# Adapter and output weights turned by VectorE and moved through DRAM, with an early reordering of the start, in a LoRA and paged-attention kernel

## The chip, the cores and the metric

The kernel runs on one core of one Trainium2 chip. The metric is the device time of one execution in microseconds (us). A core has several engines with a queue of instructions each: TensorE (PE in the profile; PEld is its weight load), VectorE (DVE), ScalarE (ACT), GpSimd (POOL) and SyncE (SP). DMA transfers are issued from the queues of SP, ACT and POOL. An engine executes its queue in order, so an instruction that waits holds up everything behind it on that engine.

## The reference, cut to what matters

For 8 batches of 128 tokens of width 512, all in float32:

```python
# layer 0: each batch has its own adapter, a 512 x 512 matrix out of 16
w = weight[adapter_ids]
x = x + einsum('bsi,boi->bso', x, w)

# layer 1: attention over a paged cache of 512 keys and the 128 new ones
q = rope(rmsnorm(x @ Wq.T, q_norm_w))      # 32 heads of 128
k = rope(rmsnorm(x @ Wk.T, k_norm_w))      # 8 heads of 128
v = x @ Wv.T
kc, vc = k_cache[block_table], v_cache[block_table]     # 16 pages of 32
scores = q . concat(kc, k) / sqrt(128), keys past the batch's length masked
o = softmax(scores) . concat(vc, v)
x = x + o @ Wo.T
```

All weights lie in DRAM with the output index first, so each 128 x 512 block of rows has to be turned (transposed) before TensorE can use it.

## The kernel before

**Steps and slots.** The work is cut into 32 steps: 4 groups of heads (g) times 8 batches (b), `steps = [(g, b) ...]`, group by group. A step handles 8 query heads and 2 key heads of one batch and has 8 slots, one for each query head. A slot begins with the matmuls of that head's scores (`sc`, line 1040; two buffers in PSUM). VectorE adds the mask and takes the minimum (L1050), ScalarE takes the exponential (L1066), VectorE inverts the sum (L1106), GpSimd scales (L1113), and one slot later VectorE turns the probabilities in blocks of 32 x 32 (`turn_p`, L886). SP's DMAs (`exchange`, L806) bring the blocks to their places (`pT`).

**The planner.** Between the score matmuls TensorE gets a list of pieces, `main`: the projections of the next step (`pj_kv`, `pj_q`), the probabilities times values of the step before (`values`, tile `o`), the output of the step before (`output`, tile `out`), and in group 0 the adapter product of a later batch (`lora_y`, tile `y`). A matmul piece has a cost of 0.86 (`UNIT`), a transpose 0.11 (`TR`). Beside them stand `turns`, transposes with a fixed slot (`at(step, slot, early, f)`; early ones come ahead of the exponential, the others after the slot's pieces). In each slot the planner hands out pieces as long as they fit its share:

```python
ahead = sum(c for k in range(h + 1, 8) for _, c, _ in turns_at.get((i, k), []))
mine = sum(t[1] for t in turns)
share = (sum(c for c, _ in main) + ahead + mine) / (8 - h) - mine
while main and (h == 7 or took + main[0][0] / 2 <= share):
```

Copies and additions that follow a group of matmuls are put into `pending` and emitted at the next `run(pending)`.

**Turning weights.** There are two ways. `turn_weights`, `turn_lora` and `turn_lora_row` use four TensorE transposes into a PSUM buffer (`ps_mm`, a ring of four; `spare` takes one of the two `sc` buffers), and one copy out of it by ScalarE or VectorE. All weights of group 0 and all adapters are turned so. The other way serves groups 1 to 3: `send_weights` has VectorE turn 32 x 32 blocks (L513) into a `facing` tile and returns the DMA that writes it to DRAM, emitted a slot later from the ACT queue (`to_write`); `receive_weights` reads it back from the same queue, many slots later. The slots of the turns stand in `turn_when`, those of the reads in `reads_at`; after each turn `load_next` fetches the next block of weights.

**Adapters.** The row of adapter numbers selects the adapter. Adapters 0 and 1 are loaded by SP; `gather_lora` (POOL, L239) gathers the others, 1 MB each, into a single buffer `lraw`. In step i of group 0 `turn_lora(i + 2, c)` turns adapter i + 2, one chunk c in each of four slots; `lora_y(i + 2)` multiplies, an addition updates `acc`, and `turn_x1(i + 2)` turns the result for the projections. `turn_x(b)` turns x itself ahead of that.

**Unused space.** The output weights of group 0 (`o0`, `o1`) wait from the start in the tiles of batches 4 to 7 (`acc`, `x1T`), until these are needed.

**The start.** Ahead of step 0 the order is written out by hand: a small row (lengths, block table, adapter numbers, norm weights) is spread over the partitions by two tiny matmuls (`spread`, L391), from it come rope tables and gather indices; x, the first weights and adapters 0 and 1 are turned, step 0 is projected, and the cached keys of step 0 are turned by TensorE (`turn_kc`, L763, copies L766).

Of the kernel before, what the change touches and what calls it, by code (L numbers as in the profile page):

```python
# [18 lines left out]
P = 128  # L19
# [33 lines left out]
def lora_then_paged_attention(  # L53
# [28 lines left out]
    facing = pool("facing", 2)  # L82
# [121 lines left out]
    wn = const.tile([P, 2, D], FP, name="wn")  # L204
# [53 lines left out]
    for i, (g, b) in enumerate(steps):  # L258
        if i == 0:
            at(i, 2, False, lambda: turn_q(0, 1))  # L260
            at(i, 7, False, lambda: turn_q(1, 0))
            for n, h in enumerate((7, 8, 9, 10)):
                at(i, h, False, lambda n=n: turn_weights(("o1", 0, n)))
# [12 lines left out]
        if g == 0 and b + 2 < B:  # L276
            at(i, 0, True, lambda b=b: turn_x(b + 2))
            for c in range(KC):
                at(i, c if i else c + 2, False, lambda b=b, c=c: turn_lora(b + 2, c))
            at(i, 8 if i else 9, True, lambda b=b: turn_x1(b + 2))  # L280
    for turns in turns_at.values():
        turns.sort(key=lambda t: not t[0])

# [6 lines left out]

    for g in range(1, G):
        before = 8 * B * (g - 1)
        for k, kind in enumerate(("kv", "q0", "q1")):
            for n in range(4):
                turn_when[before + 9 + 5 * (4 * k + n) // 2] = len(turns_of)
                turns_of.append((kind, g, n))
                read_at(before + 8 * (B - 2) + (2, 4, 6)[k] + n, (kind, g, n))
        for n, slot in enumerate((39, 42, 45, 62, 64, 66, 68, 70)):
# [95 lines left out]
    def rope_angles():  # L394
# [20 lines left out]
        nc.vector.tensor_scalar(turns, turns, ROUND, None, ALU.subtract)  # L415
        for part in (TWO_PI_1, TWO_PI_2, TWO_PI_3):
# [6 lines left out]
    def row_rest():  # L423

        nc.vector.tensor_copy(row_f[:, at_bt:at_wn], row_i[:, at_bt:at_wn])
# [26 lines left out]
    def rope_table(n):  # L452
        sin, cos = rope["sin"], rope["cos"]
        if n == 0:
# [5 lines left out]
        nc.vector.tensor_tensor(SW[:, n, :, H2:D], sin, w1, ALU.mult)  # L460
        nc.vector.scalar_tensor_tensor(
            out=SW[:, n, :, 0:H2], in0=sin, scalar=-1.0, in1=w2, op0=ALU.mult, op1=ALU.mult
        )
        nc.vector.tensor_tensor(CW[:, n, :, 0:H2], cos, w1, ALU.mult)
        nc.vector.tensor_tensor(CW[:, n, :, H2:D], cos, w2, ALU.mult)
# [7 lines left out]
    def transposed(name, blocks, dsts, copy=None, spare=False):  # L473
# [8 lines left out]
        for dst, lo, n in dsts:  # L482
            (copy or nc.scalar.copy)(dst, t[:, lo : lo + n, :])  # L483
# [26 lines left out]
    def send_weights(kind, a, n):  # L510

        t = facing.tile([P, 4, 4, Q4], FP, tag="tw", name=f"tw_{kind}_{a}_{n}")
        nc.vector.transpose(t, raw.pop((kind, a, n)).rearrange("p (c i a) -> p a c i", c=4, a=4))  # L513
# [7 lines left out]
    def receive_weights(kind, a, n):  # L521
        if n == 0:
            wT[kind] = wts.tile([P, 4, 4, 4, Q4], FP, tag=kind, name=f"w_{kind}_{a}")
        nc.scalar.dma_start(
            out=wT[kind][:, n, :, :, :].rearrange("p b c j -> p b (c j)"),
# [3 lines left out]
    def turn_lora(b, c, copy=None, spare=False):  # L529

        if c == 0:
            wT["lora"] = lora.tile([P, KC, 4, P], FP, tag="wT", name=f"wT_{b}")
# [4 lines left out]
            [(wT["lora"][:, c, :, :], 0, 4)],  # L537
# [4 lines left out]
    def turn_lora_row(b, j, copy):  # L542

        if j == 0:
            wT["lora"] = lora.tile([P, KC, 4, P], FP, tag="wT", name=f"wT_{b}")
        rows = lraw[b].rearrange("p (j i) -> p j i", j=4)
        transposed(f"lw_{b}_{j}", chunks(rows[:, j, :]), [(wT["lora"][:, :, j, :], 0, 4)], copy)


    def turn_x(b, copy=None):  # L550
        transposed(f"x_{b}", chunks(acc[b]), [(x1T[b], 0, 4)], copy)

    def turn_x1(b, copy=None):
        transposed(f"x1_{b}", chunks(acc[b]), [(x1T[b], 0, 4)], copy)
# [32 lines left out]
    def lora_y(b):  # L587
        def after(y):
            def add():
                a = acc[b].rearrange("s (p j) -> s j p", j=4)  # L590
                nc.vector.tensor_tensor(a, y.rearrange("s (j p) -> s j p", j=4), a, ALU.add)
# [6 lines left out]
                lambda c=c: (x1T[b][:, c, :], wT["lora"][:, c, :, :].rearrange("k j p -> k (j p)"))  # L598
# [334 lines left out]
    table_set(AF.Sin)  # L933
    rope_angles()
    turn_x(0, on_act)
    for n in (2, 3, 0, 1):
        turn_weights(("kv", 0, n), on_act)
    rope_sin()
# [252 lines left out]
```

## Time and profile before

| | |
|---|---|
| time, median of 3 runs | 1193.76 us (1192.11 to 1201.34) |
| the profiled execution's own time | 1193.18 us |
| its span, first to last instruction | 1191.3 us |
| TensorE busy | 1172.7 us, 98% of the span |
| VectorE, ScalarE, GpSimd busy | 743.9, 534.0, 674.1 us |
| DMA moved | 217.59 MB, mean 183 GB/s |
| first score matmul of step 0 | 40.75 us |

In lists of waits a row names who waited for whom, with the total in us, the number of times and the longest. In a timeline a row has its start, its length, engine, line, operation, `out<-in`, shapes and count, and in brackets how long the engine stood idle before it and what ended that. Rows of a timeline can overlap a little, since an engine starts the next instruction before the one ahead has drained. In a table by stage each engine's busy time in us is followed by its number of instructions. "Clock" is the granted TensorE clock, 1.00 at full speed.

### The profile page before, as it was taken

The page shows a single profiled execution, that of the slowest core. Times are in us where ns is not written, and L with a number is a line of the kernel's source. Part 1 is how long each engine was busy: PE and PEld are TensorE (multiplying, and loading weights), DVE is VectorE, ACT ScalarE, POOL GpSimd, SP SyncE. Part 2 cuts the span into 40 slices and gives each one's busy share as a digit, 9 for nine tenths or more (in the row PEclk, how much of TensorE's full clock was granted, in tenths as well). Part 3 has the DMA queues.
Part 4 walks back from the last instruction along what each step waited for, and adds up shares of the span by engine and source line. Part 5 has one row for each costly group of instructions (what it writes and reads, how often), then busy time and mean ns, then how long its engine had stood idle before and what let it go on. Part 6 is the DMA issues. An engine that isn't in the chain of part 4 may idle for free.

```text
span 1191.3 us, 13375 instructions
## 1 busy us (share of the span) xinstructions
PE 1172.7 (98%) x3354; PEld 572.0 (48%) x3354; DVE 743.9 (62%) x1675; ACT 534.0 (45%) x1648; POOL 674.1 (57%) x780
## 2 busy tenths in 40 slices
PE   7899999999999999999999999999999999999998
PEld 4555454454444444444444444444444444444454
DVE  5566566565667676666666676676666656665651
ACT  4564444444444444444444444444444444444432
POOL 5565346455666565656655556565555656655540
PEclk9999999999999999999999999999999999999999
DMA  8277577766867977786777978766777875665642
GB/s 291 100 180 197 135 220 206 172 180 168 226 173 189 253 192 191 191 215 169 199 187 180 258 198 216 196 175 171 190 203 178 219 180 148 148 153 135 152 111 59
DMA packets 173952, 217.59 MB, mean 183 GB/s; under 512 B 19508, under 2 KB 112436, under 8 KB 172980
## 3 DMA queue, kind: packets, MB, share of 16 engines
q1 hardware_dynamic: 111072, 128.76, 46.8%
q10 hardware_dynamic: 49524, 48.12, 12.7%
q0 software_dynamic: 13280, 39.86, 10.4%
q8 instruction: 28, 0.46, 0.2%
q14 instruction: 48, 0.39, 0.1%
HBM read 80.74 MB, written 17.83 MB: 83 GB/s over the span
## 4 chain that ended last, share of the span: by engine, by line
PE 96%; POOL 1%; DMA 1%; ACT 1%; DVE 1%; issue 1%; DVEq 0%; ACTq 0%; POOLq 0%
PE sc L1040 23%; PE o L566 23%; PE pj_q L566 18%; PE out L566 18%; PE pj_kv L566 9%; PE y L566 2%; PE lw L481 1%; DMA lraw<-in_L_cond_weight_dram,lora_ix 1%; PE x L481 1%; PE wt_q L499 0%; PE wt_kv L499 0%; PE qt L793 0%; PE wt_o L499 0%; POOL kc L617 0%; POOL vc L617 0%
## 5 line engine op out<-in xcount | busy, mean ns | idle before, releaser
L1050 DVE CUSTOM_DVE_ANT_0 p<-sc,mask 128x640 f32<-128x640 f32 x256 | 210.9, 824 | 381.2 <-PE sc L1040 380.9
L1066 ACT ACTIVATE p<-p,mn 128x640 f32<-128x640 f32 x256 | 212.0, 828 | 331.8 <-DVE mn L1050 328.0
L1113 POOL TENSOR_SCALAR p<-p,rc 128x640 f32<-128x640 f32 x252 | 201.5, 800 | 235.3 <-DVE rc L1106 230.9
L1040 PE MATMUL sc<-kT,qT 128*128 128x512 f32 (+1 forms) x1024 | 319.5, 434 | 1.1 <-ACT kT L773 0.8
L1040 PEld LDWEIGHTS sc<-kT,qT 128*128 128x128 f32 x1024 | 192.7, 191 | 232.5 <-issue 225.7
L566 PE MATMUL pj_q<-w_q,x1T 128*128 128x512 f32 x512 | 236.8, 593 | 0.7 <-ACT w_q L500 0.7
L566 PE MATMUL o<-pT,vc 128*128 128x512 f32 x512 | 237.1, 593 | 0.0
L566 PE MATMUL out<-w_o,oT 128*128 128x512 f32 (+1 forms) x528 | 234.9, 580 | 0.9 <-ACT oT L853 0.7
L886 DVE STREAM_TRANSPOSE tp<-p 128x640 f32<-128x640 f32 x252 | 210.8, 837 | 4.0 <-POOL p L1113 3.8
L685 POOL TENSOR_TENSOR q<-q,sw 128x512 f32<-128x512 f32 (+1 forms) x89 | 96.6, 1086 | 98.8 <-DVE sw L668 98.6
L617 POOL DMA_INDIRECT kc<-in_L_cond_k_cache_dram,key_ix x128 | 130.7, 1021 | 32.7 <-issue 32.5
L617 POOL DMA_INDIRECT vc<-in_L_cond_v_cache_dram,val_ix x128 | 127.3, 995 | 31.2 <-issue 29.8
L566 PEld LDWEIGHTS out<-w_o,oT 128*128 128x128 f32 x528 | 95.7, 190 | 93.5 <-issue 85.4
L566 PEld LDWEIGHTS pj_q<-w_q,x1T 128*128 128x128 f32 x512 | 92.4, 190 | 92.7 <-issue 90.6
L698 ACT ACTIVATE q<-q,rs 128x128 f32<-128x128 f32 x256 | 81.8, 390 | 118.1 <-POOL q L685 102.2
L566 PEld LDWEIGHTS o<-pT,vc 128*128 128x128 f32 x512 | 92.2, 191 | 88.5 <-issue 86.4
L566 PE MATMUL pj_kv<-w_kv,x1T 128*128 128x512 f32 x256 | 116.6, 593 | 0.7 <-ACT x1T L483 0.7
L651 ACT ACTIVATE sq<-pj_q 128x128 f32<-128x128 f32 x256 | 70.6, 276 | 57.5 <-PE pj_q L566 41.6
L693 POOL TENSOR_TENSOR rs<-ss,mhalf 128x6 f32<-128x6 f32 x64 | 77.3, 1207 | 5.3
L566 PEld LDWEIGHTS pj_kv<-w_kv,x1T 128*128 128x128 f32 x256 | 46.0, 190 | 45.6 <-issue 44.7
L566 PE MATMUL o<-pT,vn 128*128 128x512 f32 x128 | 65.4, 593 | 0.0
L651 ACT ACTIVATION_READ_ACCUMULATOR sq<-pj_q 128x1 f32 x256 | 49.7, 194 | 0.0
(123 smaller groups left out, 811.5 us busy)
## 6 DMA issues: line engine op xcount, KB each, us to landing
pT<-tp SPq DMA_DIRECT2D x252, 320.0 KB, 6.1
kT<-tk SPq DMA_DIRECT2D x248, 64.0 KB, 2.9
qT<-tq SPq DMA_DIRECT2D x116, 96.0 KB, 2.7
qT<-tq SPq DMA_DIRECT2D x120, 64.0 KB, 4.0
st_q<-in_L_cond_Wq_dram ACTq DMA_DIRECT2D x24, 256.0 KB, 5.5
xw_q<-tw_q ACTq DMA_DIRECT2D x24, 256.0 KB, 5.5
st_o<-in_L_cond_Wo_dram ACTq DMA_DIRECT2D x24, 256.0 KB, 5.7
xw_o<-tw_o ACTq DMA_DIRECT2D x24, 256.0 KB, 6.5
```

Of the source, the lines that this page charges most:

```text
L481: nc.tensor.transpose(t[:, j, :], blk, ident)
L566: nc.tensor.matmul(y[0], lhsT=lhsT, rhs=rhs, start=(k == 0), stop=(k == len(pieces) - 1))
L617: nc.gpsimd.indirect_dma_start(out=dst[:, c, :], out_offset=None, in_=src, in_offset=bass.IndirectOffsetOnAxis(ap=rows[:, g, at : at + 1], ...
L651: nc.scalar.activation(sq, t[:, h, :], AF.Square, scale=float(D) ** -0.5, accum_out=ss[:, h : h + 1])
L685: add.tensor_tensor(dst, cw, sw[:, 0:heads, :], ALU.add)
L693: nc.gpsimd.tensor_tensor(rs[:, 0:width], ss[:, 0:width], mhalf[:, 0:width], ALU.pow)
L698: nc.scalar.activation(q, q, AF.Identity, scale=rs[:, h : h + 1])
L886: nc.vector.transpose(u.tp[:, :, r, :], u.p.pop(r).rearrange("q (a k) -> q a k", a=4))
L1040: nc.tensor.matmul(sc[:, lo:hi], lhsT=s.qT[j][:, r, 0:4, :].rearrange("d h q -> d (h q)"), rhs=s.kT[j].rearrange("d a c i -> d (a c i)")[: ...
L1050: nc.vector.tensor_tensor_reduce(out=p, in0=sc[:, 0:LA], in1=mask.rearrange("p a c i -> p (a c i)"), scale=1.0, scalar=3.0e38, op0=ALU.add ...
L1066: nc.scalar.activation(p, p, AF.Exp, bias=unit.mn[:, one], scale=-1.0, accum_out=unit.sm[:, one])
L1113: nc.gpsimd.tensor_scalar(q, p, unit.rc[:, one], 1.0, ALU.mult, ALU.mult)
```

## The change

- **The start.** x of batch 0 and two blocks of kv weights are turned ahead of the first small spread, and two rows of adapter 0 ahead of the second. The sine and cosine tables come after the gather of keys; `rope_table(1)` is split into its sine and cosine halves. The last two q1 weight blocks are turned between the kv and the q0 projection; the q1 projection and its `run(pending)` now stand ahead of the key gather of step 1 and of `turn_kc`. `row_tables` and the mask move later.
- **Step 0.** The four o0 blocks come one after the other, `turn_x1(1)` after all of them.
- **Adapters 4 to 7 and o1 of group 0** go through `send_weights` and `receive_weights`, in the slots of `extra`; each read stands two slots after its write. Adapter 3 stays with TensorE, two chunks a slot. The adapter's turned tile gets the layout of the other weights, `[P, 4, 4, KC, Q4]`.
- **Around it.** `gather_lora(b + 3)` moves from the end of slot 6 to the end of slot 2, `load_x(b + 3)` to slot 4 (step 0 keeps slot 6); `turn_x1(7)` comes a slot earlier; turns of group 1's weights move to slots that `extra` leaves free; `facing` has three buffers, and `wn` shares the tile `tk`.

```diff
@@ turns
+            at(i, 6, False, lambda: row_tables(range(1, G)), 0)
             at(i, 7, False, lambda: turn_q(1, 0))
-            for n, h in enumerate((7, 8, 9, 10)):
-                at(i, h, False, lambda n=n: turn_weights(("o1", 0, n)))
...
-            for c in range(KC):
-                at(i, c if i else c + 2, False, lambda b=b, c=c: turn_lora(b + 2, c))
-            at(i, 8 if i else 9, True, lambda b=b: turn_x1(b + 2))
+            if i < 2:
+                for c in range(KC):
+                    at(i, c // 2 if i else c + 2, False, lambda b=b, c=c: turn_lora(b + 2, c))
+            at(i, (7 if b + 3 == B else 8) if i else 9, True, lambda b=b: turn_x1(b + 2))
@@ slots of turns and reads
+    extra = {}
+    for n, slot in enumerate((5, 6, 7, 8)):
+        extra[slot] = ("o1", 0, n)
+        read_at(slot + 3, ("o1", 0, n))
+    for b in range(4, B):
+        for j, slot in enumerate((8, 8, 9, 10)):
+            extra[8 * (b - 3) + 4 + j] = ("lora", b, j)
+            read_at(8 * (b - 3) + slot, ("lora", b, j))
...
+                if g == 1:
+                    slot = (9, 10, 11, 17, 18, 24, 25, 26, 32, 33, 34, 40)[4 * k + n]
...
-        for n, slot in enumerate((39, 42, 45, 62, 64, 66, 68, 70)):
+        for n, slot in enumerate((42, 44, 46, 62, 64, 66, 68, 70)):
@@ send_weights, receive_weights
-        nc.vector.transpose(t, raw.pop((kind, a, n)).rearrange("p (c i a) -> p a c i", c=4, a=4))
+        rows = lraw[a][:, n * HID : (n + 1) * HID] if kind == "lora" else raw.pop((kind, a, n))
+        nc.vector.transpose(t, rows.rearrange("p (c i a) -> p a c i", c=4, a=4))
...
+            pl, tag = (lora, "wT") if kind == "lora" else (wts, kind)
+            wT[kind] = pl.tile([P, 4, 4, 4, Q4], FP, tag=tag, name=f"w_{kind}_{a}")
+        dst = wT[kind][:, :, n, :, :] if kind == "lora" else wT[kind][:, n, :, :, :]
@@ start
     row_parts()
     table_set(AF.Sin)
+    turn_x(0, on_act)
+    for n in range(2):
+        turn_weights(("kv", 0, n), on_act)
     rope_angles()
-    turn_x(0, on_act)
-    for n in (2, 3, 0, 1):
+    for n in range(2, 4):
         turn_weights(("kv", 0, n), on_act)
-    rope_sin()
+    for j in range(2):
+        turn_lora_row(0, j, on_act)
     row_rest()
-    for j in range(4):
+    for j in range(2, 4):
         turn_lora_row(0, j, (on_act, on_vec)[j % 2])
...
     for _, f in project(0, "kv"):
         f()
+    for n in range(2, 4):
+        turn_weights(("q1", 0, n), on_act)
     rope_table(0)
     run(pending)
     for _, f in project(0, "q0"):
         f()
+    make_mask(0)
     run(pending)
-    for j in range(GK):
-        turn_kc(0, j, on_vec)
-    for n in range(2, 4):
-        turn_weights(("q1", 0, n), on_act)
+    for _, f in project(0, "q1"):
+        f()
     run(pending)
     for c in range(LC):
         gather_k(1, c)
-    row_tables(range(1, G))
-    for _, f in project(0, "q1"):
-        f()
+    for j in range(GK):
+        turn_kc(0, j, on_vec)
     turn_x(1, on_vec)
     for c in range(KC):
         turn_lora(1, c, on_vec if c % 2 else on_act, True)
     gather_lora(2)
+    turn_k(0, 0, on_act)
     turn_q(0, 0, on_act)
-    turn_k(0, 0, on_act)
@@ step 0 and the loop
-                if n == 2:
+                if n < 4:
+                    turn_weights(("o0", 0, n))
+                else:
                     turn_x1(1)
-                turn_weights(("o0", 0, n))
-            main += [(4 * TR * (1 + n // 2), lambda n=n: second(n)) for n in range(3)]
-            main += [(4 * TR, lambda: turn_weights(("o0", 0, 3)))]
+            main += [(4 * TR, lambda n=n: second(n)) for n in range(5)]
...
+            if 8 * i + h in extra:
+                to_write.append(send_weights(*extra[8 * i + h]))
...
-            if g == 0 and h == 6 and b + 3 < B:
-                load_x(b + 3)
-                gather_lora(b + 3)
+            if g == 0 and b + 3 < B:
+                if h == (4 if i else 6):
+                    load_x(b + 3)
+                if h == (2 if i else 6):
+                    gather_lora(b + 3)
```

## Prediction

> **What bounds it now.** I read the busy shares first, then the waits of TensorE (PE), then busy time by stage, then the timelines of PE and VectorE (DVE) at the start.
>
> ```profile
> PE 1172.7 (98%) x3354; PEld 572.0 (48%) x3354; DVE 743.9 (62%) x1675; ACT 534.0 (45%) x1648; POOL 674.1 (57%) x780
> ```
>
> PE is busy for all but 18.6 us of the span. Only two things can shorten the kernel: instructions taken from PE, and the few waits that PE has. They stand in the list of waits (total, times, longest):
>
> ```profile
> PE spread L391 <- DVE row_f L395: 6.1, 1, 6.1
> PE lw L481 <- DMA lraw<-in_L_cond_weight_dram,lora_ix: 2.4, 1, 2.4
> PE x L481 <- DVE rc L1106: 0.9, 1, 0.9
> ...
> PE pj_kv L566 <- ACT x1T L483: 0.7, 1, 0.7
> ```
>
> The start of each step (its first sc matmul in PE's timeline) gives stages: the first at 40.75, step 0 33.4 us long, step 1 42.0, step 2 44.7, steps 3 to 5 40.5 each, step 6 35.8, and 34.4 from step 7 on. Columns are PE, PEld, DVE, ACT, POOL busy, clock, DMA share, GB/s; the rows are steps 2, 3 and 9:
>
> ```profile
> 116.13:160.87 44.74, 42.34 (x126) 21.10 (x125) 25.57 (x53) 18.33 (x55) 21.55 (x25) 0.96 0.65 178
> 160.87:201.33 40.46, 40.46 (x125) 20.18 (x124) 25.29 (x55) 18.42 (x55) 21.53 (x25) 1.00 0.74 194
> ...
> 386.85:421.25 34.40, 34.40 (x93) 16.23 (x92) 23.59 (x52) 15.01 (x49) 19.63 (x23) 1.00 0.93 249
> ```
>
> Step 3 has no idle PE at all, so what is taken from PE there is time. Step 2 loses 4.27 us against it: 2.40 of waiting for the gathered adapter, and the rest by the clock, which is 0.5 for 3.41 us after that wait. Its matmuls show it: four of sc take 2.34 us, elsewhere 1.24.
>
> ```profile
> 123.22 1.03 PE L481 MATMUL lw<-ident,lraw 128*128 128x128 f32 x4 [2.40 <-DMA lraw<-in_L_cond_weight_dram,lora_ix]
> 124.05 2.34 PE L1040 MATMUL sc<-kT,qT 128*128 128x512 f32 x4
> ```
>
> **Term A, adapters 4 to 7 leave PE: -7.0.** In each of steps 2 to 5 four groups of four transposes go; a group moves the next instruction by 0.436 us (lw at 129.88, sc at 130.32). 16 x 0.436 = 7.0. In exchange come, for these and the o1 rows of term B, 20 turns on DVE, 20 writes and 20 reads on the ACT queue.
>
> - DVE: 20 x 1.06 us (L513) = 21 us, 4.2 a step. It is busy 25.3 of 40.46 us in step 3 and waits 1 to 3 us a slot for sc; with 29.5 of 38.7 it still fits, and the fullest slot (rotation, mask, p turn and one weight turn, 198.10 to 202.39) took 4.3 us. Price 0.
> - DVE may wait for the gather: it is issued after slot 2's p, 6.1 us into that slot, and lands 5.8 to 9.1 us later (rows of lraw); the turn in slot 4 comes some 13.3 us after slot 2's start. That is 0 to 2 us, with the reciprocal and the next mask operation queued behind. PE is a slot ahead in two sc buffers: 0.
> - ACT loses 20 copies of 0.585 us and gets 40 issues, 0.33 for a write, 0.37 to 3.06 for a read. A read waits for its write; two slots are 9 us, the longest such write took 7.4. Behind a late one stand the exp and all that follows it. In steps 7 to 30 such reads run with no PE wait: 0.
> - DMA: the ACT queue took 12.7% of the span for 48.12 MB, 3.1 us per MB; 2.1 MB more in a step of 38.7 us is 0.17. 0.74 x 40.5/38.7 + 0.17 = 0.94. Step 9 ran at 0.93 without a PE wait: 0, but this is the edge, and rival 2.
> - Moves: the gather goes ahead of the two key gathers of slot 3 on POOL, 0.94 + 0.3 us of issue; x (0.4 us on SP) goes ahead of the pT transfer of slot 5 instead of the next step's. Each has slots to spare: 0.
>
> **Term B, second output weights (o1) leave PE: -1.3.** Four groups of 0.436. The three in step 1 count. The one that closed step 0 covered the qT copy of the next step: sc waited 0.24 us there with it, and waits 0.68 without.
>
> **Term C, the wait of step 2: -4.3.** Adapter 4 is no longer PE's; 44.74 goes to 40.47 before term A. **Term D, step 6: -0.7**, because x1 of batch 7 is turned a slot earlier, ahead of its kv projection.
>
> **Term E, the start: +2.5.** PE's first transposes can begin at some 4.0 (x and the first weights land at 3.9 and 4.8), not 6.06, but adapter 0's second half lands at 12.3 whatever the order, so y starts near 14.05 instead of 15.44. With two more weight turns now ahead of q0, the q0 projection ends at 29.05 (29.41 before) and q1 right after, at 32.55 (36.61 before): 4 us gained on PE. Then the new order bites. Before, q1's rotation ran in slot 0; now it stands ahead of the kct copies on DVE, and a rotation starts only when ACT's squares are done:
>
> ```profile
> 31.09 0.69 DVE L664 TENSOR_TENSOR q<-pj_q,CW 128x512 f32<-128x512 f32 x1 [3.20 <-ACT sq L651]
> 31.70 0.74 DVE L668 TENSOR_TENSOR sw<-pj_q,SW 128x256 f32<-128x256 f32 x2
> 32.48 0.69 DVE L685 TENSOR_TENSOR q<-q,sw 128x512 f32<-128x512 f32 x1
> 33.08 1.28 DVE L766 COPY kT<-kct 128x512 f32<-128x512 f32 x2
> ```
>
> Queue by queue, from 29.05: ACT squares q0 to 30.7; DVE rotates it (2.08) to 32.8; ACT scales it (1.28) to 34.2 and squares q1 (1.56) to 35.8; DVE rotates q1 to 37.9, copies kct (1.28) to 39.1, x (0.62) to 39.8, adapter 1's second chunk (0.65) to 40.4; PE turns the fourth chunk, which needs that buffer, to 40.9, then k and q; ACT copies both to 42.15. So sc starts at 42.15, +1.4. PE idles 3.5 us before that fourth chunk; after 2.40 us the clock halved, so I add 1.1 for turns and sc at half clock. Bounds: -4.1 (all of the q1 gain kept) to +3.5 (3.41 us at half clock cost 1.7 on top of 1.4, plus 0.4 for the later gathers).
>
> **Term F, step 0: +1.6.** The planner in the loop hands PE its pieces by cost. In slot 1 it now has one y piece and five 0.44 turns. Before, the test passed for all (2.84 against 20.12/7 = 2.874); with the o1 turn gone the share is 19.68/7 = 2.811, and x1 of batch 1 falls into slot 2, directly ahead of the kv projection that reads it. Its copy is queued on ACT behind the exp of slot 2: mask 1.29 us after the slot's start, exp at 2.15, copy 2.98 to 3.56, kv at 3.65; PE is ready at 1.75. Wait 1.9. In slot 1 the fourth o0 turn needs the buffer that the y addition frees: 0.6. The old 0.93 wait goes. 1.9 + 0.6 - 0.9 = 1.6. Whether 1.9 us also halves the clock (+1.7) lies between two rows: 0.93 did not, 2.40 did; I take no. Bounds: -0.9 to +3.3.
>
> [...]
>
> **Term G, adapter 3 in step 1: +1.0.** It is still PE's, now both first groups in slot 0, and no o1 turn stands ahead. Before, it landed at 78.20 and was used at 78.77. Without the 0.44 the margin is 0.1 us, and the writes of o1 share the DMA: one 256 KB write is about 1 us. Bounds 0 (landing in 5.8) to 5.0 (in 9.1: 3.3, and 1.7 of clock).
>
> **Term H, adapter 7: +0.3.** In step 5 its y comes in slot 3, 6.46 us after slot 2's start; its last read is issued at 2.25 in slot 2 and lands 4.3 to 4.8 us later (w_q, w_o). Bounds 0 to 2.
>
> **Sum.** -7.0 - 1.3 - 4.3 - 0.7 + 2.5 + 1.6 + 1.0 + 0.3 = -7.9. The profiled execution took 1193.18 us (span 1191.3), 0.6 under the median of the runs, 1193.76. 1193.2 - 7.9 = 1185.3. About 1% is what a measurement of this kernel can tell from no change: faster is below 1181.8, slower above 1205.7.
>
> **Rivals.**
> 1. *The start pays* (chance 0.21). The DVE chain of term E overlaps better than I queue it and 3 of the 4 us stay; x1's copy is in time. -13.3 - 3.0 + 0.5 = -15.8: 1177.4. For it: q1 ends 4 us earlier. Against: the order on DVE and ACT is in the code.
> 2. *The round trip is late* (0.07), the other side. From slot 2's read to y are 8.8 us for adapters 4 to 6, 4.2 for 7. If reads take 12 us, PE waits 3 x 3.2 + 7.8 = 17.4 and each of four waits costs 1.7 of clock: 1185.3 + 17.4 + 6.8 = 1209.5. For it: a DMA share of 0.94 over five steps in a row. Against: step 9, and no weight read or write above 7.4.
> 3. *The moved turns bound DVE* (0.07): steps 2 to 5 stay at 40.5 because a slot's DVE work passes the slot, so term A does not appear. 1185.3 + 7.0 = 1192.3. Against: 29.5 of 38.7.
>
> [...]
>
> **Chances.** Forecast 0.65, rivals 0.21, 0.07, 0.07. Faster by over 1%: rival 1 and 0.04 of the forecast's own spread, 0.25. Slower by over 1%: 0.06 of rival 2. Within: 0.69. The bounds add to 1175 and 1194; both ends at once are unlikely below, so the range is 1178 to 1194.
>
> **What would show it.** Right: steps 3 and 4 last 38.7 us with full PE, no lw wait in step 2, the first sc near 42 to 43.5 with an idle PE before the fourth lw of adapter 1, a kv wait for x1T in slot 2 of step 0 near 1.9, few tenths at lw in step 1. Wrong: a first sc before 40, PE waits for wT in steps 2 to 5, DVE waits there that reach sc.

## The result and the profile after

The changed kernel takes 1208.05 us (median of 4 runs, 1205.59 to 1210.23) against 1192.98 for the kernel before on the same chip: a ratio of 1.0113, 95% interval 1.0087 to 1.0139 (the medians alone give 1.0126). It is slower by 1.1%, where 1185.3 was forecast, in a range of 1178 to 1194. Its profiled execution took 1205.59 us (span 1203.8), 12.4 more than the 1193.18 of before.

The engines' line of the page after:

```profile
PE 1171.9 (97%) x3274; PEld 565.7 (47%) x3274; DVE 757.4 (63%) x1694; ACT 522.8 (43%) x1629; POOL 673.1 (56%) x780
```

TensorE has 80 instructions fewer, but only 0.8 us less busy time: once the clock has first been full, five stretches of 3.41 us at half clock (from 14.76, 42.06, 86.44, 144.46 and 229.80 us) lengthen its matmuls, where the kernel before had one (from 123.30). The span is longer by 12.5 us, and 31.9 us of it are idle, 18.6 before. The waits of PE after (total, times, longest):

```profile
PE o L590 <- DMA pT<-tp: 5.7, 3, 2.5
...
PE lw L498 <- DMA lraw<-in_L_cond_weight_dram,lora_ix: 2.7, 1, 2.7
PE o L590 <- issue: 2.4, 1, 2.4
PE y L590 <- DMA w_lora<-xw_lora: 2.2, 1, 2.2
...
PE pj_kv L590 <- ACT x1T L501: 1.8, 1, 1.8
PE sc L1069 <- ACT kT L803: 1.6, 1, 1.6
```

Before, `o` (probabilities times values) did not wait at all. Now it waits in each of steps 1 to 4, 0.73, 2.41, 2.40 and 2.52 us, for `pT`, the probabilities that VectorE has turned and SP's DMAs spread. (The 2.40 stands under "issue", as the trace shows no event at its end.) Steps 2, 3 and 9 by stage, with PE, PEld, DVE, ACT, POOL, clock, DMA share and GB/s:

```profile
125.07:168.13 43.06, 40.65 (x110) 19.11 (x108) 27.49 (x58) 16.12 (x51) 21.56 (x25) 0.96 0.81 218
168.13:209.47 41.34, 38.94 (x109) 18.54 (x108) 28.33 (x59) 16.24 (x51) 21.52 (x25) 1.00 0.85 238
...
399.33:433.73 34.40, 34.40 (x93) 16.23 (x92) 23.48 (x52) 15.11 (x49) 19.54 (x23) 1.00 0.92 251
```

Step 3 has 38.94 us of PE work where 38.7 was forecast, but lasts 41.34. From step 7 on nothing differs: step 7 starts at 318.04 us before and at 330.53 after. By stage, against before:

| stage | forecast | measured |
|---|---|---|
| start and step 0 (E, F) | +4.1 | +4.8 |
| step 1 (B, G) | -0.3 | +4.2 |
| steps 2 to 4 (A, C) | -9.5 | +1.9 |
| step 5 (A, H) | -1.4 | +2.9 |
| step 6 (D) | -0.7 | -1.3 |

**Why `pT` can be late.** A step's probabilities come in two units, and up to step 4 both use one buffer of `pT`. Until the values of the first unit have been multiplied, SP cannot issue the second. SP's rows in step 3 before (start 160.87) and after (168.13):

```profile
164.95 2.51 SPq L806 DMA_DIRECT2D qT<-tq  x4
168.83 5.53 SPq L806 DMA_DIRECT2D pT<-tp  x4
```

```profile
172.22 2.49 SPq L831 DMA_DIRECT2D qT<-tq  x4
175.65 5.04 SPq L831 DMA_DIRECT2D pT<-tp  x4
```

SP begins 8.0 us after the step's start before, 7.5 after. PE wants the result 17.7 us after the start before:

```profile
178.54 1.88 PE L566 MATMUL o<-pT,vc 128*128 128x512 f32 x4
```

It landed at 17.1 to 17.3 in steps 3 to 5, so in steps 3 and 4 the margin was about half a microsecond (in step 5 PE wants it later). After, without the adapter's transposes, PE is there at 16.5 us, and the landing has moved to about 18.8. Counted from the issue, PE leaves 9.0 us instead of 9.7, and the transfer takes 11.2 and 11.5 in steps 2 and 4 instead of 9.2 to 9.3. So 0.7 us of the wait are the transposes that PE no longer does meanwhile, and the larger part is the slower transfer. The wait of step 2, which starts at 125.07:

```profile
144.00 4.51 PE L590 MATMUL o<-pT,vc 128*128 128x512 f32 x6 [2.41 <-DMA pT<-tp]
```

(144.00 is 18.93 us after 125.07; six matmuls take 4.51 us at a clock of 0.50 from 144.46 on, where they take 2.81 in step 3.) The DMA engines in these 11 us (7.5 to 18.5 of step 3), by queue with packets, MB and share; q1 is SP's queue, q10 ScalarE's. Before, then after:

```profile
DMA packets 1216, 2.01 MB, mean 183 GB/s; under 512 B 135, under 2 KB 440, under 8 KB 1216
...
q1 hardware_dynamic: 920, 1.47, 64.3%
q10 hardware_dynamic: 296, 0.54, 12.8%
```

```profile
DMA packets 2165, 2.78 MB, mean 253 GB/s; under 512 B 161, under 2 KB 1208, under 8 KB 2161
...
q1 hardware_dynamic: 704, 1.37, 56.1%
q10 hardware_dynamic: 1457, 1.38, 37.6%
```

ScalarE's queue moves 1.38 MB there instead of 0.54, and the share of all queues goes from 77% to 95%, while over the whole step after it is 85%.

### The profile page after: what moved, and what is told of

Read it like the earlier page. It is cut to its first block, busy times and chain, and to the rows that moved or that the text cites. A ratio compares the mean times of both kernels' runs of the same rounds, so it can differ in the third digit from the quotient of the medians.

```text
span 1203.8 us, 13251 instructions
## 1 busy us (share of the span) xinstructions
PE 1171.9 (97%) x3274; PEld 565.7 (47%) x3274; DVE 757.4 (63%) x1694; ACT 522.8 (43%) x1629; POOL 673.1 (56%) x780
## 4 chain that ended last, share of the span: by engine, by line
PE 89%; DMA 5%; SPq 1%; DVE 1%; POOL 1%; issue 1%; ACT 1%; ACTq 0%; POOLq 0%; DVEq 0%
PE o L590 23%; PE sc L1069 22%; PE out L590 18%; PE pj_q L590 16%; PE pj_kv L590 8%; DMA pT<-tp 3%; PE y L590 2%; SPq L831 1%; DMA lraw<-in_L_cond_weight_dram,lora_ix 1%; DMA qT<-tq 1%; DMA raw_lora<-in_L_cond_weight_dram 1%; DMA w_lora<-xw_lora 1%; PE x L498 0%; POOL kc L642 0%; SPq L160 0%
## 5 line engine op out<-in xcount | busy, mean ns | idle before, releaser
L590 PE MATMUL o<-pT,vc 128*128 128x512 f32 x512 | 240.0, 600 | 8.1 <-DMA pT<-tp 5.7
L717 POOL TENSOR_SCALAR ss<-ss 128x6 f32<-128x6 f32 x64 | 13.0, 203 | 69.2 <-ACT sq L676 67.7
```

Of the source, the lines that this page charges most:

```text
L590: nc.tensor.matmul(y[0], lhsT=lhsT, rhs=rhs, start=(k == 0), stop=(k == len(pieces) - 1))
L717: nc.gpsimd.tensor_scalar(ss[:, 0:width], ss[:, 0:width], EPS, 1.0, ALU.add, ALU.mult)
```

## Experiments

Where no ratio is given the time is that of one execution; the kernel before took 1191.54 us beside the first four runs (e1 to e3) and 1191.19 beside e4 to e7. Single times of one and the same kernel differ by up to 12 us (f1, below), so what these runs tell is read from the waits in their profiles.

### Which traffic makes pT late

**e1_no_gather**: VectorE turns a constant, and adapters 4 to 7 are not gathered.

```diff
-        rows = lraw[a][:, n * HID : (n + 1) * HID] if kind == "lora" else ...
+        rows = key_no.rearrange("p a c j -> p (a c j)") if kind == "lora" else ...
-                    gather_lora(b + 3)
+                    if b == 0:
+                        gather_lora(b + 3)
```

> The changed kernel without the gathers of adapters 4 to 7: VectorE turns a constant in their place, everything that follows (writes, reads, products) is kept, so batches 4 to 7 get a wrong adapter. In the changed kernel the pT transfer of unit 1 in steps 2 to 4 starts 7.5 us into the step, when the values of unit 0 have been read out of the single pT buffer, and lands at 18.7; TensorE is ready for it at 16.5 and waits 2.4. The 1 MB gather starts at 15.2, in the middle of this transfer. Theory 'moved gather': the transfer shrinks to the 9.2 us of before, the waits fall to 0.2 to 0.5, steps 2 to 4 take about 39 us instead of 43.1, 41.4, 43.2, the whole about 1195. Theory 'round trip': the writes and reads in slots 0 to 2 slow the transfer, the gather does not, the waits stay at 2 to 2.4.

1205.94 us. The waits of steps 1 to 4 stay: 1.33, 1.98, 2.65, 2.28. Without the gather ScalarE's queue still moves 0.95 to 1.43 MB in the 11 us.

**e1b_no_gather_two_buffers**: the same, and the first unit's `pT` in the adapter's idle buffer, so that the second need not wait for it.

```diff
-        pl, tag = (lora, "raw") if u.j == 0 and u.i >= B - 3 else (pts, "pT")
+        pl, tag = (lora, "raw") if u.j == 0 and u.i >= 1 else (pts, "pT")
```

> As e1, and pT of unit 0 goes into the adapter's buffer, free without the gathers, from step 1 on, so that the two units have a buffer each. Theory 'single buffer': the transfer of unit 1 starts as soon as its last turn is done, about 3 us into the step instead of 7.5, lands by 13, and the waits of steps 2 to 4 are gone whatever the traffic is: 38.7 us each. If the transfer were late for another reason (SP's queue, VectorE's turns), it would not start earlier and the waits would be those of e1.

1207.38 us; waits of 0.91, 0.53, 2.44, 4.13. SP starts only 0.9 us sooner (6.63 against 7.52), since its exchange of the next step's `qT` stands ahead. The single buffer is not what decides.

**e2_no_traffic**: the adapters are gathered and turned, but not written and read back (the products use what is in the tile).

```diff
-                to_write.append(send_weights(*extra[8 * i + h]))
+                key = extra[8 * i + h]
+                write = send_weights(*key)
+                if key[0] != "lora":
+                    to_write.append(write)
...
-                receive_weights(*key)
+                if key[0] != "lora":
+                    receive_weights(*key)
```

> The changed kernel without the writes to DRAM and the reads of adapters 4 to 7 (gathers and VectorE's turns stay; the products use adapter 3's tile, so batches 4 to 7 are wrong). Theory 'round trip': the unit 1 transfer takes 9.2 us again, waits of 0.2 to 0.5 in steps 2 to 4, which take about 39 us. Theory 'moved gather': the waits stay at 2 to 2.4. Both theories: the wait for adapter 7's reads in step 5 (2.2) is gone. If the shorter cover alone were at fault (9.0 us of TensorE work between the units instead of 9.75), neither e1 nor e2 would change the waits.

1200.33 us. The wait of step 5 is gone, but those of steps 1 to 4 remain: 0.85, 1.97, 2.83, 1.83. The gather and group 1's weights, whose turns the change had moved together, are enough.

**e4_before_plus_traffic**: the kernel before with dummy writes and reads.

```diff
+            if 8 * i + h in dummy_write:      # steps 1 to 3, slots 5, 6, 7, 0
+                nc.scalar.dma_start(out=d_dram[k]..., in_=key_no...)
+            for k in dummy_read.get(8 * i + h, []):      # slots 0, 0, 1, 2
+                nc.scalar.dma_start(out=idle_tile..., in_=d_dram[k]...)
```

> The kernel before, with eight more writes and eight more reads of 256 KB on the ACT queue in steps 1 to 3, in the slots in which the changed kernel moves adapters 4 and 5; the data moved is a constant, and what is read lands in idle tiles that nothing uses. Nothing else is changed: the adapters stay on TensorE. Theory (the transfer pT of unit 1 is late because the DMA engines are full in the 9 us between its issue and its need): it landed 0.45 us ahead of its need before, so 1 MB more in that window makes PE wait in the values of steps 2 and 3, 0.5 to 2 us each, 1 to 5 us in all with the clock; the DMA share from 7.5 to 18.5 us of these steps goes from 0.66 to 0.77 up to 0.85 to 0.95. Rival (the cover is what counts: with the adapters' transposes gone the values come 0.75 us sooner, and the traffic matters little): no wait for pT, 0 to 0.3 us, since the transposes are still there.

1203.01 us; PE waits 1.59 us for `pT` in step 2 and 1.11 in step 3, none in 4 and 5, where nothing was added. Step 2 from 7.5 to 18.5 us of it, and its wait (the row names the releaser "kT", but it is the same matmul on `pT`):

```profile
128.60:139.60 11.00, 11.00 (x37) 5.64 (x37) 5.42 (x13) 4.82 (x13) 1.60 (x2) 1.00 0.85 223
```

```profile
142.03 1.96 PE L571 MATMUL o<-pT,vc 128*128 128x512 f32 x4 [1.59 <-DMA kT<-tk]
```

So the traffic alone makes the wait, with the transposes still on PE: from issue to landing the transfer takes 11.2 and 10.7 us in steps 2 and 3, and 9.2 in step 4. Against the profiled execution of the kernel before (1193.18) the run is 9.8 us longer. Of these 4.7 are the start (first score at 45.49), which is the same code as before and is taken up below; in step 3 the gathered adapter came 2.34 us late as well, and the clock was low beside it (a mean of 0.84 from 7.5 to 18.5 us of the step).

**e5_old_slots**: the changed kernel with group 1's turns in their old slots.

```diff
-                if g == 1:
-                    slot = (9, 10, 11, 17, 18, 24, 25, 26, 32, 33, 34, 40)[4 * k + n]
```

> The changed kernel with the turns of group 1's weights back in the slots of the kernel before (9, 11, 14, 16, 19 and so on), so that their writes and reads no longer gather in slots 0 to 3; the adapters still go through DRAM. Theory (both streams together fill the window of pT): waits for pT in steps 2 to 4 fall from 2.4 us to 1 to 1.8, no drop of the clock, 1202 to 1205. Rival (the round trip of the adapters alone fills it): waits of 2 us and more, 1206 to 1209. Rival (the regrouped weights alone do it): waits under 0.8, 1198 to 1201.

1208.26 us; waits of 0.74, 2.06, 1.41, 3.71. My theory that it takes both streams fell: the round trip and the gather are enough without the regrouped weights.

**e6_none**: e1, e2 and e5 together. TensorE's and VectorE's work is that of the changed kernel.

> The changed kernel without the gathers of adapters 4 to 7, without the writes and reads of their turned blocks (VectorE turns a constant instead, and the products read whatever an earlier adapter left), and with the turns of group 1's weights in the slots of the kernel before. VectorE's and TensorE's work is that of the changed kernel. Theory (full DMA engines): the transfer lands 17.2 us after the step's start as before, the need is at 16.5, so 0 to 0.8 us of waiting in each of steps 2 to 4, no drop of the clock, these steps 38.7 to 39.5 us, 1194 to 1198 in all with the same start. Rival (the shorter cover, or the work of VectorE, whatever the DMA does): waits of 1.5 us and more, steps 2 to 4 above 40.5.

1194.52 us; waits in steps 2 to 4 of 0.05, 0.02 and 0.00 (step 1, where o1's blocks still move, keeps one of 1.16). Step 3:

```profile
167.33:206.29 38.96, 38.94 (x109) 18.54 (x108) 28.38 (x59) 16.24 (x51) 20.52 (x24) 1.00 0.67 173
```

Step 4 lasts 38.71. This is the forecast of term A, and no run here had it with the bytes. `pT` now lands 16.2 to 16.4 us after the step's start: with fewer bytes beside it, it is early enough even for the earlier PE. VectorE at 28.5 us a step bounds nothing, which rules out rival 3.

**e3_q1_first**: the changed kernel, the projection of q1 ahead of the second unit's values.

```diff
-        if i and not early:
-            main += values(i - 1, 1)
-        if b + 3 < B:
+        if early or b + 3 >= B:
+            if i and not early:
+                main += values(i - 1, 1)
+            if i < last:
+                main += project(i + 1, "q1")
+        else:
+            main += project(i + 1, "q1")
+            if i:
+                main += values(i - 1, 1)
             main += first
-        if i < last:
-            main += project(i + 1, "q1")
```

> The changed kernel with the q1 projection ahead of the values of unit 1 in steps 1 to 4, which puts four more pieces (3.4 us) and most of a slot's sc between the two units. Theory 'single buffer and its cover': cover grows from 9.0 to 12.4 us and more, above the transfer's 11.1, and the waits in steps 1 to 4 are gone (0.7, 2.4, 2.4, 2.5, with the half clock after two of them): steps 2 to 4 take 38.7 to 39 us, the whole about 1194. The adapter's wait in step 1 (2.65) and those of steps 0 and 5 stay. If the transfer is held by what TensorE does, it would move with the pieces and the waits would stay.

1207.42 us. `o` no longer waits, but the first score of the next steps does, 1.4 to 2.9 us, for `qT` and `kT`: the values end later, so the next `pT` leaves later (158.17 us, 5.84 of issue), and the exchange of `qT` stands behind it on SP's queue (164.12, 7.56 of issue, with the score at 173.47). The wait was moved along the queue.

### Whether another place in the step helps

**f4_start_undone_retimed**: the old start; gather, turns and reads elsewhere.

```diff
-        for j, slot in enumerate((8, 8, 9, 10)):
+        for j, slot in enumerate((7, 7, 8, 9)):
-            extra[8 * (b - 3) + 4 + j] = ("lora", b, j)
+            extra[8 * (b - 3) + (3 if b > 4 else 4) + j] = ("lora", b, j)
...
+            if g == 0 and 1 <= i and b + 4 < B and h == 7:
+                gather_lora(b + 4)
```

> The changed kernel with the old start, and the traffic of the adapters moved out of the time in which pT is under way: the gather issued at the end of slot 7 of the step ahead (adapter 4: slot 3), VectorE's turns in slots 3 to 6, their reads in slots 7, 7, 0 and 1, group 1's weights turned in slots 7, 0 and 1; x of batch 1 is turned after two of the four o0 blocks, and adapter 3's turns stand a slot later. Theory (pT is late because the DMA engines are full from 7.5 to 18.5 us of the step): waits for pT below 1 us, none above, steps 2 to 5 at 38.7 to 39.7 us, no wait for x1T in step 0, 1180 to 1187 in all. If the waits stay above 1.5 us, it is not the traffic in that window that counts but what the step moves in all.

1207.01 us (ratio 1.0119, 1.0094 to 1.0144). I had read the place wrong. GpSimd runs behind TensorE: it issued the gather of "the end of slot 7" 8.1 us into step 2 and 4.8 us into steps 3 and 4, and the gather's 1 MB now ran beside `pT`. The 11 us of step 3 (share 1.00), and its wait:

```profile
171.10:182.10 11.00, 9.02 (x24) 3.88 (x23) 7.22 (x16) 5.16 (x21) 2.35 (x4) 1.00 1.00 290
```

```profile
186.37 5.33 PE L589 MATMUL o<-pT,vc 128*128 128x512 f32 x6 [6.25 <-DMA kT<-tk]
```

With 1.99 MB on the other queues beside `pT` instead of 1.41 (step 3) the waits are 5.43, 6.25 and 5.14 us instead of 2.4 to 2.5: the dose confirms the cause, though the variant was meant to cure it.

**g1_clear_window**: the gather two slots earlier still, so that it lands ahead of the 11 us.

```diff
-                if h == (2 if i else 6):
+                if i < 2 and h == (2 if i else 4):
                     gather_lora(b + 3)
+            if g == 0 and 1 <= i and b + 4 < B and h == 5:
+                gather_lora(b + 4)
...
+        # turned in slots 3, 4, 5, 5 (adapter 4: 4, 4, 5, 5), read in 6, 7, 8, 8
```

> The changed kernel with the old start, the same bytes through DRAM, and the adapters' traffic placed by what GpSimd's and ScalarE's own timelines show: adapters 5 to 7 are gathered at the end of slot 5 of the step ahead (on GpSimd some 5 us before the step starts, landing near 4), turned by VectorE in slots 3, 4, 5, 5, written a slot later and read in slots 6, 7 and 0; adapter 3 is gathered and turned earlier, group 1's weights are turned in slots 6, 7 and 0, and x of batch 1 after two of the o0 blocks. Theory (the place of the traffic counts): ACT's queue moves under 0.5 MB from 7.5 to 18.5 us, pT waits under 0.5 us in steps 3 to 5 (step 2 up to 1.5), these steps 38.7 to 39.3 us, 1179 to 1187 in all. Rival (the sum counts: the same bytes in a step of 38.7 us fill the engines wherever they stand): waits of over 1 us for pT, or as much for the new keys at the step's end, 1190 and above.

1216.96 us (ratio 1.0205, 1.016 to 1.0251), the slowest of all. Its premise did not come about: ScalarE's queue moved 1.03 to 1.76 MB in the 11 us of steps 2 to 4 where I expected under 0.5. `pT` waits 5.11, 2.68 and 2.01 us there, and the next step's first score waits up to 3.5 us for `kT`. Whether some placement of these bytes would hide them all is therefore open; two attempts failed, and neither had the traffic where it was meant to be.

### The gather alone, in the kernel before

Four runs of the kernel before with one number changed, the slot after which it issues its gather (6 there); batch 7's x is turned a slot earlier in all four.

```diff
-            if g == 0 and h == 6 and b + 3 < B:
-                load_x(b + 3)
-                gather_lora(b + 3)
+            if g == 0 and b + 3 < B:
+                if h == 6:
+                    load_x(b + 3)
+                if h == (N if i else 6):        # N = 4, 5, 3
+                    gather_lora(b + 3)
```

What was expected of f3, g2, g3 and h3, in this order:

> The kernel before with two edits only: the gather of adapters 4 to 7 is issued at the end of slot 4 instead of slot 6, and x of batch 7 is turned a slot earlier. Adapters and weights stay on TensorE and nothing goes through DRAM that did not. The terms C and D of the prediction alone: step 2 from 44.7 to 40.5, step 6 from 35.8 to 35.1, 1188 to 1189.5. If the earlier gather is in the way of pT, which has 0.45 us to spare, waits for pT appear in steps 1 to 4 and the time is 1191 or above.

> The kernel before with its gather issued at the end of slot 5 (slot 6 before, slot 4 in f3) and x of batch 7 turned a slot earlier. In f3 the gather ran beside the exchange of the new keys, and the next step's first score waited 1.8 us for kT after steps 2 and 4, as much as was won. Here the gather starts some 4.5 us later than in f3, with the keys mostly through: no lw wait in step 2, kT waits under 0.5 us, 1188 to 1191. If the exchange is later than I read, kT waits as in f3 and 1193 to 1195.

> The same with the gather at the end of slot 3: it starts near 21 us of the step, behind pT (landed at 17) and ahead of the exchange of the new keys. No wait for lw, pT or kT, step 2 at 40.5, 1187.5 to 1190. If kT still waits, 1193 to 1195.

> The kernel before with the gather of adapters 4 to 7 at the end of slot 3 and x of batch 7 a slot earlier, once more (g3: 1190.1, ratio 0.9977). Terms C and D say -5; in g3 step 2 took 40.5 as it should. If that holds, 1187.5 to 1190.5 and a ratio of 0.995 to 0.999, its interval below 1.

| gather after slot | median us | ratio (95%) |
|---|---|---|
| 4 (f3) | 1194.19 | 1.0007 (0.9989 to 1.0025) |
| 5 (g2) | 1200.80 | 1.0055 (1.0030 to 1.0080) |
| 3 (g3) | 1190.08 | 0.9977 (0.9954 to 1.0000) |
| 3 (h3) | 1191.11 | 0.9981 (0.9966 to 0.9996) |

The 5.0 us of terms C and D did not come: h3 missed its range by 0.6, g3 by 0.1, f3 and g2 by 5 and 10. All three slots remove the `lw` wait of step 2, but after slots 4 and 5 the first score of the next step waits for `kT`, 1.76 and 3.61 us. The gather's issue on GpSimd and the exchange of `kT` on SP, f3 (start of step 3 at 160.28) and then g3 (157.29), a GpSimd row and an SP row each:

```profile
145.12 1.09 POOL L239 DMA_INDIRECT lraw<-in_L_cond_weight_dram,lora_ix  x1 [0.17 <-issue]
...
156.24 3.40 SPq L806 DMA_DIRECT2D kT<-tk  x4
```

```profile
139.97 0.95 POOL L239 DMA_INDIRECT lraw<-in_L_cond_weight_dram,lora_ix  x1 [0.30 <-PE o L566]
...
154.05 2.49 SPq L806 DMA_DIRECT2D kT<-tk  x4
```

In f3 the gather is under way up to 155.97, 10.8 us. `kT` is issued at 156.24, 2.3 us before PE is ready for the step (158.52), and its issue takes 3.40. In g3 the gather is through at 147.06; `kT` starts 3.2 us before PE wants it and takes its usual 2.49. (In the kernel before, the gather was issued at 158.55, with `kT` already on its way since 157.62.) g3's step 2 is what term C forecast:

```profile
116.83:157.29 40.46, 40.46 (x125) 20.18 (x124) 25.55 (x52) 18.45 (x55) 21.37 (x25) 1.00 0.67 200
```

This version beats the kernel before, by 0.2%.

### The start, the o1 rows, and the clock

**e7_start_undone** and **f2_start_undone_again** are one kernel: the changed one, with the whole start of the kernel before (from `row_parts()` to the last turn of the start) and without

```diff
-            at(i, 6, False, lambda: row_tables(range(1, G)), 0)
```

Two words of the texts below, as the profiles show them: a drop is a stretch at half clock, and the grid is the row of borders on which these stretches lie. In the profile of the changed kernel each of the five is 3.41 us long and starts a whole multiple of that length (3.413 us) after the one ahead of it. Cut into such lengths, its span has its first border at 1.10 us, and that of the kernel before, through its one stretch, at 0.42.

> The changed kernel with the start of the kernel before, all of it, the row tables included; from step 0 on it is the changed kernel. This prices the new order of the start. First score matmul at 40.6 to 40.9 (42.4 changed, 40.75 before); step 0 35.5 to 36.5 us, as the late copy of x of batch 1 stays; steps 1 to 6 as in the changed kernel within 1 us each; 1204 to 1207 in all. If instead the new start is worth something that the later steps hide, the time is that of the changed kernel or above.

> The changed kernel with the start of the kernel before, once more: its one profile had four waits for pT (1.4, 1.9, 2.8, 2.1 us) and no window at half clock, 1193.5. Theory (that was the grid): here some of the waits halve the clock, 1195 to 1200 in the median, and the new start proper costs the rest, 6 to 10 us against the unaltered changed kernel. Rival (the old start shifts the phase for good): 1193 to 1194 in every run, and the new start is worth 12 us.

**f1_changed_again** is the changed kernel without an edit.

> The changed kernel once more, unaltered. [...] Rival (the drops belong to the kernel, and the single runs of the variants differ by their edits): drops at the same places, all times within 2 us of 1206.

e7 had one execution, 1193.54 us, 12 less than the changed kernel, and from that alone the start would have cost 12. Over 12 runs f2 has a median of 1199.16 (1197.35 to 1209.61; ratio to before 1.0059, 1.0038 to 1.0080). f1 has 1206.12 over 6 runs, 1198.99 to 1210.81 (1.0100, 1.0063 to 1.0137). The difference of the medians is 7.0; up to the start of step 1 the two profiles differ by 2.8 (78.88 against 76.06). The mean clock scatters with the times: f1's two fastest runs have 0.997 and 0.996, its other four 0.993 or 0.994. Here are two waits for `pT` in the changed kernel, in step 2 and in step 3, with the rows cut at the borders of that grid, in windows of 3.41 us. The first column after the length is PE's busy time, the third from the end the clock:

```profile
141.05:144.46 3.41, 1.00 (x3) 0.30 (x2) 1.62 (x5) 0.80 (x2) 2.45 (x4) 1.00 1.09 304
144.46:147.88 3.42, 3.42 (x5) 1.33 (x4) 0.00 (x0) 1.47 (x8) 2.51 (x4) 0.50 0.93 309
182.01:185.42 3.41, 2.64 (x8) 0.98 (x6) 2.10 (x8) 1.91 (x7) 1.92 (x3) 1.00 0.96 214
185.42:188.84 3.42, 1.79 (x5) 0.87 (x5) 0.60 (x2) 0.64 (x4) 2.87 (x4) 1.00 1.07 363
188.84:192.25 3.41, 3.41 (x11) 1.74 (x10) 1.27 (x3) 1.18 (x7) 2.08 (x3) 1.00 1.03 361
```

The wait of 2.41 us lies in one window, which leaves PE 1.00 us of work, and the next window runs at half clock. The wait of 2.40 us in step 3 lies across a border; the two windows keep 2.64 and 1.79 us, and the clock stays at 1.00. In e7 a wait of 2.83 us left its two windows 2.28 and 1.73 us, and there too it stayed at 1.00. In the two kernels' profiles, from 45 us of the span to step 7, the full-clock windows with half clock behind them had 0.77, 1.00 and 1.28 us of PE work (changed kernel, from 83.02, 141.05 and 226.38 us) and 1.02 (kernel before, from 119.88); none of the others had less than 1.79. At the start, where PE mostly transposes, windows with 2.33 and 1.73 us had half clock behind them as well (changed kernel, from 11.34 and 38.65), so PE's work in the window does not by itself tell which it will be. The changed kernel's profile has three half-clock windows after waits of steps 1 to 4; the mean clock of the profiled execution is 0.993 there and in f1, 0.997 in f2 and 1.000 in e7. The one behind the wait of step 2 cost 1.7 us: the same six matmuls take 4.51 us behind the wait of step 2 and 2.81 behind that of step 3. f1's times were to lie within 2 us of 1206 by its rival, and lie 11.8 us apart: the rival is out. But a part of the 7.0 is still unexplained by the two profiles, and with 6 and 12 runs that scatter so it stays open.

**h1_o1_only** and **h2_o1_new_start** leave the adapters on TensorE and keep only o1 in DRAM, with the old and the new start; otherwise they are alike.

```diff
-            if i < 2: ...
+            for c in range(KC):
+                at(i, c if i else c + 2, False, lambda b=b, c=c: turn_lora(b + 2, c))
...
-    for b in range(4, B):
-        for j, slot in enumerate((8, 8, 9, 10)): ...
...
-                if h == (2 if i else 6):
+                if h == (3 if i else 6):
                     gather_lora(b + 3)
...
-            main += [... for n in range(5)]
+            main += [... for n in (0, 1, 4, 2, 3)]
```

> The changed kernel with the old start, adapters 4 to 7 back on TensorE (one chunk a slot), their gather at the end of slot 3, group 1's weights in the slots of the kernel before, x of batch 1 after two of the o0 blocks. Only the four o1 blocks of group 0 go through DRAM: terms B, C and D. Against g3 term B alone is added: -1.3, 1188 to 1190. If the 2 MB more in steps 0 and 1 are in the way of adapter 3's gather or of pT, a wait of 0.5 to 3 us in step 1 eats it: 1190 to 1194.

> h1 with the new start, the row tables in slot 6 of step 0 included. This is term E alone. By the profiles so far: first score 0.5 to 1.7 us later, a half-clock window on it in most runs (1.7), so h1 plus 2.5 to 3.5 us. If the start costs what the medians of the changed kernel with and without it differ by, h1 plus 5 to 7. If h2 is as fast as h1, the new start costs nothing and the difference came from the waits behind it.

h1: 1192.51 us (0.9986, 0.9970 to 1.0003). It should have been 1.3 below h3, which ran beside it, and is 1.4 above. With the 2 MB for o1 beside it the gather of adapter 3, issued at 72.00, is waited for up to 81.02; in the kernel before it was issued at 72.40 and landed at 78.20:

```profile
81.02 0.63 PE L490 MATMUL lw<-ident,lraw 128*128 128x128 f32 x4 [2.09 <-DMA lraw<-in_L_cond_weight_dram,lora_ix]
```

h2: 1196.17 us (1.0030, 1.0015 to 1.0045), 3.7 above h1, and by the start of step 1 the profiles differ by 3.6 (77.31 against 73.71). The first score in h1, then in h2:

```profile
40.33 1.35 PE L1057 MATMUL sc<-kT,qT 128*128 128x512 f32 x4 [0.84 <-ACT kT L790]
```

```profile
41.43 2.50 PE L1062 MATMUL sc<-kT,qT 128*128 128x512 f32 x4 [0.68 <-ACT qT L812]
```

It comes 1.1 us later and at half clock (2.50 us for 1.35), after waits of 1.51, 0.68 and 0.47 us. Term E's 2.5 was short by about one, and rival 1, a start that pays, fell.

## Why the prediction was wrong

- **The failed step is term A's line on the DMA engines: 0.94 of share over the step, price 0, since step 9 ran at 0.93 without a wait.** The average over a step was the wrong measure (it came to 0.81 to 0.85, and PE waited all the same). What counts is the stretch in which `pT` is under way. In the 11 us from 7.5 to 18.5 of steps 3 and 4 the kernel before stood at 0.77 and 0.67, with about half a microsecond to spare, and the change took the engines to 0.95 and 0.96. Step 9 was no guide. There SP issues this `pT` 3.7 us after the step's start (386.85) and PE takes it 20.0 us after it:

```profile
390.58 5.75 SPq L806 DMA_DIRECT2D pT<-tp  x4
...
406.85 1.88 PE L566 MATMUL o<-pT,vc 128*128 128x512 f32 x4
```

  That is 16 us of room where steps 2 to 4 have 9. The engines were as full there, 0.94 while `pT` was under way, and it took 12.9 us to land (403.47); in 9 us of room PE would have waited for it. I had read that step 9 hid its traffic, and not from what. e4 (bytes without the change) and e6 (the change without bytes) show the cause from both sides. It cost 7.3 us of waits in steps 2 to 4 and 3.4 of clock (PE is busy for 40.65 and 40.68 us in steps 2 and 4, for 38.94 in step 3), of the 11.4 missed there.
- **Term A's size, 7.0, was right** (38.94 us of PE in step 3; e6's steps 2 to 4 last 39.00, 38.96 and 38.71, for 38.7), and so was VectorE's price of 0.
- **Terms C and D were right in the profile, and too large for most runs**: the `lw` wait of step 2 went, and step 6 got 1.3 shorter (0.44 of it four transposes that now stand in step 5). Alone they measured 1.9 us and not 5.0 (g3, h3). In g3 step 1 lasts 0.7 longer; and 49 of the 71 runs of the kernel before beside f1 to h3 have a mean clock of 1.000, so they did not lose the half-clock window that makes 1.9 us of term C and that the profiled execution had. The moved gather was priced only by GpSimd's issue. Its 1 MB runs beside or just ahead of `pT` or `kT`, and g2 and g3 show 11 us between one slot and another; what of it holds up `kT` was not separated.
- **Term B's 1.3 was taken back in step 1**, where term G was mis-sized: the wait for adapter 3 was 2.65 us and a half-clock window (from 86.44, 1.7), together 4.4 for the 1.0 chosen, inside its bounds of 0 to 5.0. h1 has the o1 rows without the rest and lost the same way.
- **Term E** was right in its chain: first score at 42.42 for 42.15, and half clock (2.47 us for the four matmuls that take 1.24 in step 0's next slot); PE's idle time there came in four pieces (1.51, 0.68, 0.47, 0.90) and not in one of 3.5 before the fourth chunk. Its size was 2.5; h1 and h2 give 3.7.
- **Term F** held: 1.80 us at `pj_kv` for 1.9, 0.49 for 0.6; and the next step's `sc` waited 0.68, as term B has it.
- **Term H** was 2.2 us where 0.3 was taken and 2 was the bound. e2, without the round trip, has no such wait. The 1.6 us for `kT` at the end of that step were not foreseen, and what made them was not tried.
- **Rival 2 named nearly the right time, 1209.5, by a mechanism that did not occur**: adapters 4 to 6 were never late for their products, only 7 was.

## What to carry to other kernels

Before traffic is called hidden, find the transfer with the least margin, take its stretch from issue to need out of the timelines, and price the new bytes in that stretch: here a share of the DMA engines over a whole step said nothing of it (0.85 in step 3 of the changed kernel, with a wait of 2.40 us), nor did another step with a longer stretch (0.92 in its step 9, without one). Place a transfer by the time at which its own engine's queue reaches it, which here was 5 to 8 us after the slot in the code. And work that is taken from the bounding engine also takes away the cover of whatever it was waiting behind.

## What the runs showed of the hardware that I had not expected

- The longer wait was not the dearer one: behind a wait of 1.98 us the six matmuls of `o` took 4.51 us (e1, step 2), behind one of 2.65 us 2.81 (e1, step 3). What decides it was not shown.
- The start scatters too. With the very same start code the first score came at 40.75 us in the kernel before and at 45.49 in e4. The first full clock came 10.7 us into the span of the kernel before and 7.9 into that of the changed one, whose start differs. What decides the moment was not tried.
- More bytes beside `pT` did not slow it in proportion: 0.54 and 0.83 MB on the other queues in the 11 us made no wait (before, e6), 1.4 MB made 2.4 us (after, step 3), and 2.0 MB made 6.3 (f4, step 3). The share by itself is no sharp mark: 0.86 made no wait in e6's step 3, and 0.85 and 0.76 made one in e4's steps 2 and 3, where an earlier wait had already made the transfer start 1.5 and 4.2 us later. Nor is it the number of packets: 1844 in f4's 11 us, 2165 in those of the changed kernel, which waited less.
